# Two graph layers on Trainium2: layer 1's target factor moves from the values into ScalarE's exponential of the adjacency, head by head

## The chip, the cores and the metric

One core of one Trainium2 chip runs the whole program. The metric is the device time of one execution in microseconds. A profile is one further execution, recorded instruction by instruction; its span is the time from the first to the last recorded instruction. TensorE multiplies matrices, ScalarE applies functions and copies, VectorE and GpSimd work element by element, SyncE (SP) issues most of the transfers.

## The reference: what is computed

There are 64 graphs of 256 nodes with 512 features. Two layers of attention follow each other; "layer 0" is the first, and the second layer holds two attentions, here called "layer 1" (8 heads) and "layer 2" (1 head).

```python
# layer 0
scores = einsum('bihd,bjhd->bhij', Q, K) / 8 + a[i] + c[j] + log(adjacency + 1e-9)
x = softmax(scores) @ V + x
# layer 1 and layer 2, each on a normalised input
h = layer_norm(x) @ W
s, t = h . a_src, h . a_dst                  # one number per node and head
e = leaky_relu(s[i] + t[j], 0.2) + adjacency
x = softmax(e) @ h + x
```

With the leaky slope 0.2, exp(e) can be written as a product. Up to a factor that depends on the row i alone, and that the softmax divides out, it is `max(exp(-0.8 s_i), exp(0.8 t_j)) * exp(0.2 t_j) * exp(adjacency_ij)`. The first factor is called R (one row per head, the same on all partitions), `exp(0.8 t)` is called f, and `exp(0.2 t)` is the target factor.

## The kernel before, in words

**Tiles.** Targets j lie on the partitions, in two halves (NT = 2, 128 each), and sources i along the free axis (256). Weights of four heads make one tile `ET` of 128 x 2 x 4 x 256 (line 664); each graph makes two for layer 0 (`scores0`, lines 565 to 584) and two for layer 1 (lines 662 to 673). All share the tag `ET` with four buffers. A fresh pair for layer 1 therefore takes the buffers that "product 0" gives back, the product of layer 0's weights and values of the graph behind it.

**Order of the work.** `graph(b)` (line 456) is a generator; each `yield` closes a step. The lists `start`, `period` and `finish` (lines 752 to 825) put the steps of neighbouring graphs into one written order, in which up to six graphs are under way. TensorE follows this order to the letter (`manual_schedule` for PE, line 831). VectorE, ScalarE, GpSimd and SP get their order when the program is built, from a scheduler; once built it is fixed, and each engine takes its instructions strictly one after the other.

**Products with fixed weights** go through `winograd` (lines 293 to 343): seven products instead of eight, in three PSUM banks a, b and c. The order is product 1 into a, 5 into b, 2 into c, 6 added to a, 3 added to b, 7 added to a, then 4. Before product 6 adds to a, ScalarE must have copied m (`m1`) out of a; before product 3 it must have copied `m5` out of b; before product 7 it must have copied `u2` out of a. For the query these copies are `keep_q` (line 539), two instructions each.

**Layer 1**, the stage of the change:
- "V1", "V1 7", "V1 4" (lines 615 to 640) make the values V1 and, in eight more columns per half, the numbers s and t (`ends`). The copies of V1 are scaled with `rstd`, which comes from `var` on VectorE (line 273) and a power on GpSimd (line 275).
- "rows 1" (lines 642 to 660): `target_rows` writes `exp(-0.8 s)` to DRAM and loads it back on all partitions as two tiles R of four heads (512 KB each, line 452, two buffers). ScalarE makes f, and the target factors `exp(0.2 t)` in `factors` (line 650). VectorE multiplies V1 by them (line 657).
- eight steps "weights" (lines 669 to 673), one per head: VectorE computes `max(R, f) * EA` into ET, where `EA = exp(adjacency)` comes ready-made from line 497.
- "sums 1": `weight_sums` (line 359). The weights are summed over the targets by TensorE. Since they lack the target factor, the left operand holds the factors, and each half of the targets needs its own matmul: 4 rounds x 2 halves x 4 heads = 32 matmuls (line 370), each in a quarter of the array's columns. The reciprocal (line 377) goes to DRAM and back, spread over the partitions.
- "product 1", "gather 1": `weigh` (line 392) multiplies weights and scaled values (line 403), then VectorE applies the reciprocal and adds (lines 412, 417).

**Layer 0** in "sums 0" calls `weight_sums` too, with a sum of both halves made by VectorE first (line 599) and a left operand of ones: 16 matmuls.

**Layer 2** ("rows 2", line 715) scales EA with its factor on ScalarE, in place, and its weights (line 720) are the last reader of EA. EA has four buffers. AT, the transposed adjacency plus 1e-9, has one and is used by layer 0's mask alone (line 594). The transposes of the adjacency are at line 480.

Of the kernel before, what the change touches and what calls it, by code (L numbers as in the profile page):

```python
# [9 lines left out]
F32 = mybir.dt.float32  # L10
AF = mybir.ActivationFunctionType
ALU = mybir.AluOpType
AX = mybir.AxisListType

P = 128
H = 8
# [4 lines left out]
def kernel(  # L21
# [24 lines left out]
    nc = tc.nc  # L46
    B, N, D = x.shape
    KC = D // P
    NT = N // P
    DH = D // H  # L50
# [29 lines left out]
    def sum_columns(name, n):  # L80
        t = const.tile([P, 24 + 32 * n], F32, name=name)
        nc.gpsimd.memset(t, 0.0)
        return t, t[:, 24:].rearrange("p (n c) -> p n c", c=32)[:, :, :8]

    ones, eights = sum_columns("ones", 1)
    nc.gpsimd.memset(eights, 1.0)

    factor_columns = [sum_columns(f"factors{i}", NT * H) for i in range(2)]
    filled = [None, None]

    sources = {}
    for heads in (H, 1):
# [10 lines left out]
    HD = D // 2  # L103
# [44 lines left out]
    with ExitStack() as main:  # L148
        data = main.enter_context(tc.tile_pool(name="data", bufs=1))
        work = main.enter_context(tc.tile_pool(name="work", bufs=2))  # L150
        small = main.enter_context(tc.tile_pool(name="small", bufs=2))
# [204 lines left out]
                nc.vector.tensor_reduce(worst, bad, AX.X, ALU.max)  # L356
                nc.vector.tensor_tensor(odd, odd, worst, ALU.max)

        def weight_sums(terms):

            pt = ps("su")
            for i in range(4):
                for term in terms:
                    for g in range(4):
                        columns, at, weights = term(2 * g + i // 2)
                        nc.tensor.matmul(  # L370
                            pt[32 * g : 32 * g + 32, :P], columns[:, at - 8 * i : at - 8 * i + 32],
                            weights[:, i % 2 * P : i % 2 * P + P],
                            start=(i == 0 and term is terms[0]),
                            stop=(i == 3 and term is terms[-1]),
                        )
            inverse = small.tile([P, P], F32, name="inverse", tag="inverse", bufs=1)
            nc.vector.reciprocal(inverse, pt[:, :P])  # L377

            kept = dram.tile([2 * H, P], F32, name="kept", tag="keptsums")
            nc.sync.dma_start(out=kept, in_=inverse.rearrange("(i r) n -> i r n", r=8)[:, 0, :])  # L380

            R = data.tile([P, 2, N], F32, name="R", tag="Rs", bufs=2)
            heads_of = kept.rearrange("(a q s) n -> a q (s n)", a=4, q=2)
            for a in range(4):
                nc.sync.dma_start(
                    out=R[32 * a : 32 * a + 32], in_=heads_of[a].partition_broadcast(32)
                )
            nc.vector.tensor_tensor(top[:, :P], top[:, :P], pt[:, :P], ALU.max)
            nc.gpsimd.tensor_tensor(added, added, inverse, ALU.add)  # L389
            return R  # L390

# [30 lines left out]
        def target_rows(st, heads, b):  # L422

            if heads == 1 and b == B - 1:

                e = small.tile([P, NT], F32, name="last_rows", tag="last_rows")
                nc.scalar.activation(e, st[:, :, 0, 0], AF.Exp, scale=-0.8)
                wide = data.tile([P, NT, P], F32, name="wide", tag="R1")
                nc.vector.tensor_copy(wide, e.unsqueeze(2).to_broadcast([P, NT, P]))
                pt = ps("row")  # L430
                for t in range(NT):
                    nc.tensor.matmul(
                        pt[:, t * P : (t + 1) * P], wide[:, t, :], ident, start=True, stop=True
                    )
                return [pt[:, :N].rearrange("p (h n) -> p h n", h=1)]
            e = sources[heads][b % len(sources[heads])]
            nc.scalar.activation(e[:, :, :heads], st[:, :, 0, :], AF.Exp, scale=-0.8)
            rows = small.tile([P, NT, 32], F32, name="rows", tag="rows", bufs=1)
            nc.vector.transpose(rows, e)
            kept = dram.tile([H, N], F32, name="kept", tag="kept")  # L440
            for a in range(4):
                nc.sync.dma_start(
                    out=kept.rearrange("h (t a r) -> a h t r", t=NT, a=4)[a, :heads],
                    in_=rows[32 * a : 32 * a + heads],
                )
            got = []
            for q in range(0, heads, 4):
                n = min(4, heads - q)
                R = data.tile(
                    [P, n, N], F32, name="R", tag="R" if n == 4 else "R1", bufs=2 if n == 4 else 1  # L450
                )
                nc.sync.dma_start(out=R, in_=kept[q : q + n, :].partition_broadcast(P))
                got.append(R)
            return got

        def graph(b):
# [26 lines left out]
            for t in (1, 0):  # L483
# [1 line left out]
                    xT[:, :, t * P : (t + 1) * P].rearrange("p k (a r) -> p a k r", a=4),  # L485
                    X.rearrange("p (a t) (k r) -> p t a k r", t=NT, k=KC)[:, t],
                )
            AT = data.tile([P, NT, N], F32, name="AT", tag="AT")
            EA = data.tile([P, NT, N], F32, name="EA", tag="EA", bufs=4)

            def turn_adj():
                for j in range(NT):
                    turn(
                        AT[:, j, :].rearrange("p (t a r) -> p a t r", t=NT, a=4),
                        A.rearrange("p (a t) (j r) -> p j a t r", t=NT, j=NT)[:, j],
                    )
                nc.scalar.activation(EA, AT, AF.Exp)  # L497
                nc.scalar.activation(AT, AT, AF.Identity, bias=eps)

            if b > 0:  # L500
# [85 lines left out]
            pair = [scores0(0)]  # L586
# [4 lines left out]
            totals = []  # L591
            for ET, tag in zip(pair, ("QT", "KT")):
# [6 lines left out]
                nc.vector.tensor_tensor(total, ET[:, 0], ET[:, 1], ALU.add)  # L599
                totals.append(total)  # L600
                yield
            R = weight_sums([lambda h: (ones, 24, totals[h // 4][:, h % 4])])
            xT = fetch(stored, "yT")
            yield

# [9 lines left out]
            V1 = values("V1", 2)  # L615
# [21 lines left out]
            ends = small.tile([P, NT, 2, H], F32, name="ends", tag="ends")  # L637
# [4 lines left out]
            R = target_rows(ends, H, b)  # L642
            targets = ends[:, :, 1, :]
            f = small.tile([P, NT, H], F32, name="f", tag="f")
            nc.scalar.activation(f, targets, AF.Exp, scale=0.8)

            factors, factors8 = factor_columns[b % 2]
            filled[b % 2] = b
            for j in range(NT):
                nc.scalar.activation(  # L650
                    factors8[:, j * H : (j + 1) * H, :],
                    targets[:, j].unsqueeze(2).to_broadcast([P, H, 8]), AF.Exp, scale=0.2,
                )
                for n in range(2):
                    v = V1[:, j, n, :HD].rearrange("p (h d) -> p h d", d=DH)
                    at = j * H + n * H // 2
                    nc.vector.tensor_tensor(
                        v, v, factors8[:, at : at + H // 2, :1].to_broadcast([P, H // 2, DH]), ALU.mult
                    )
            note(ends.rearrange("p t i h -> p (t i h)"))  # L660
            yield
            pair = []
            for q in range(2):
                ET = work.tile([P, NT, 4, N], F32, name="ET1", tag="ET", bufs=4)
                pair.append(ET)
                for h in range(4):
                    at = 4 * q + h
                    for j in range(NT):
                        nc.vector.scalar_tensor_tensor(  # L669
                            ET[:, j, h, :], R[q][:, h, :], f[:, j, at : at + 1], EA[:, j, :],  # L670
                            ALU.max, ALU.mult,
                        )
                    yield
            assert filled[b % 2] == b
            R = weight_sums([
                lambda h, j=j: (factors, 24 + 32 * (j * H + h), pair[h // 4][:, j, h % 4])
                for j in range(NT)
            ])
            xT = fetch(stored, "xT" if last else "zT")
            yield  # L680
            for _ in weigh(pair, V1, R, xT, folded["1"].column):
# [21 lines left out]
            ends = small.tile([P, NT, 2, 1], F32, name="ends2", tag="ends2")  # L703
# [5 lines left out]
            R = target_rows(ends, 1, b)  # L709
            f = small.tile([P, NT], F32, name="f2", tag="f2")  # L710
            nc.scalar.activation(f, ends[:, :, 1, 0], AF.Exp, scale=0.8)
            factor = small.tile([P, NT], F32, name="factor", tag="factor")
            nc.scalar.activation(factor, ends[:, :, 1, 0], AF.Exp, scale=0.2)
            for j in range(NT):
                nc.scalar.mul(EA[:, j, :], EA[:, j, :], factor[:, j : j + 1])
            note(ends.rearrange("p t i h -> p (t i h)"))
            yield
            ET = work.tile([P, NT, N], F32, name="ET2", tag="ET2", bufs=1)
            for j in range(NT):
                nc.vector.scalar_tensor_tensor(  # L720
                    ET[:, j, :], R[0][:, 0, :], f[:, j : j + 1], EA[:, j, :], ALU.max, ALU.mult
                )
            yield
            rinv = small.tile([P, NT], F32, name="rinv2", tag="rinv2")
# [372 lines left out]
```

## Time and profile before

| | |
|---|---|
| median of 3 runs | 3311.77 us (3309.73 to 3312.42) |
| span of the profiled execution | 3309.9 us |
| TensorE busy (matmul) | 3241.0 us, 98% |
| VectorE busy | 2434.1 us, 74% |
| ScalarE busy | 1453.7 us, 44% |
| GpSimd busy | 924.0 us, 28% |
| layer 1's weights (L669, VectorE) | 463.6 us, 1024 instructions |
| layer 1's sum matmuls (L370, factors) | 4096 |
| scaling of V1 (L657, VectorE) | 141.2 us, 256 instructions |

A line such as `L669 DVE ... ET<-R,f,EA ... x1024` names the source line, the engine (PE TensorE, PEld its weight load, DVE VectorE, ACT ScalarE, POOL GpSimd, SPq SyncE's queue), the tile written and those read, and how many instructions there were. In a timeline a row is one instruction or several like ones in sequence: start, length from the first start to the last end, engine, line, count; a bracket at the end gives the idle time before it and what ended it. Neighbours on one engine overlap a little, so the spacing of starts is shorter than the duration. Ends of matmuls are modelled; their starts are the better measure.

### The profile page before, as it was taken

To read this page: it belongs to the slowest core of one execution; us is meant where nothing else is said; L and a number is where in the kernel's file an instruction comes from. 1 tells how busy PE (TensorE), PEld (TensorE's weight loads), DVE (VectorE), ACT (ScalarE), POOL (GpSimd) and SP (SyncE) were. 2 spreads that over 40 slices of the span, in tenths; PEclk is the share of its full clock that TensorE was granted. 3 is DMA by queue.
4 is the path that set the end of the run, shared out by engine and by line. 5 is a ranking of instruction groups with operands and counts; after the bars stand their busy time and mean duration, and the time that the engine had idled before them with its cause. 6 is when DMAs were issued, how large, how long until landed. Compare 5 with 4: busy or idle time off the path is not lost.

```text
span 3309.9 us, 80363 instructions
## 1 busy us (share of the span) xinstructions
PE 3241.0 (98%) x31048; PEld 2745.3 (83%) x31048; DVE 2434.1 (74%) x5267; ACT 1453.7 (44%) x4039; POOL 924.0 (28%) x1246
## 2 busy tenths in 40 slices
PE   6899999999999999999999999999999999999997
PEld 4688888888888888888888888888888888888875
DVE  5677777777777777777777777777777777777776
ACT  2344444444444444444444444444444444444442
POOL 2232232232222322322322322322222223223222
PEclk9999999999999999999999999999999999999998
DMA  4323334334334333333333343343343333343322
GB/s 122 109 84 115 102 97 113 105 89 120 105 91 118 105 93 113 95 108 111 92 113 105 94 114 103 93 116 106 89 119 101 95 113 102 101 113 94 108 90 70
DMA packets 271667, 341.14 MB, mean 103 GB/s; under 512 B 108576, under 2 KB 187568, under 8 KB 271280
## 3 DMA queue, kind: packets, MB, share of 16 engines
q1 hardware_dynamic: 270512, 335.40, 35.4%
q8 instruction: 248, 4.06, 0.5%
q14 instruction: 139, 1.14, 0.1%
q10 hardware_dynamic: 768, 0.54, 0.1%
HBM read 233.48 MB, written 102.31 MB: 101 GB/s over the span
## 4 chain that ended last, share of the span: by engine, by line
PE 95%; DVE 2%; DMA 1%; SPq 1%; issue 1%; ACT 0%; POOL 0%; ACTq 0%; DVEq 0%; POOLq 0%
PE ps_a L309 21%; PE ps_a L316 13%; PE ps_num L403 13%; PE ps_b L309 10%; PE ps_b L316 7%; PE ps_sc L573 7%; PE ps_av L732 7%; PE ps_su L370 6%; PE ps_c L309 5%; PE ps_tr L252 4%; PE ps_c L316 3%; SPq L120 1%; DVE ET L669 0%; POOL product L180 0%; DMA kept<-inverse 0%
## 5 line engine op out<-in xcount | busy, mean ns | idle before, releaser
L669 DVE SCALAR_TENSOR_TENSOR ET<-R,f,EA 128x256 f32<-128x256 f32 x1024 | 463.6, 518 | 135.8 <-PE ps_num L403 134.5
L403 PE MATMUL ps_num<-ET,V 128*32 128x256 f32 x8192 | 465.9, 379 | 0.0
L403 PEld LDWEIGHTS ps_num<-ET,V 128*32 128x32 f32 x8192 | 263.5, 110 | 154.9 <-issue 0.8
L594 DVE TENSOR_TENSOR ET<-ET,AT 128x1024 f32<-128x1024 f32 x256 | 304.2, 1222 | 108.3 <-ACT ET L580 108.3
L580 ACT ACTIVATE ET<-ps_sc,V 128x512 f32<-128x512 f32 x512 | 303.3, 703 | 102.1 <-PE ps_sc L573 88.9
L389 POOL TENSOR_TENSOR added<-added,inverse 128x128 f32<-128x128 f32 x128 | 69.9, 546 | 921.7 <-DVE inverse L377 764.3
L309 PE MATMUL ps_a<-w,S 128*128 128x264 f32 (+1 forms) x1024 | 273.3, 389 | 0.9 <-ACT m L618 0.9
L309 PE MATMUL ps_b<-w,S 128*128 128x264 f32 (+1 forms) x1024 | 266.6, 383 | 0.0
L285 POOL TENSOR_TENSOR S<-yT 128x256 f32<-128x256 f32 x64 | 66.1, 1033 | 670.2 <-PE ps_su L370 595.6
L732 PE MATMUL ps_av<-V,ET 128*128 128x258 f32 (+1 forms) x1024 | 245.5, 383 | 7.2 <-DVE ET L720 7.2
L573 PE MATMUL ps_sc<-QT,KT 64*128 64x256 f32 x2048 | 238.6, 383 | 0.0
L309 PEld LDWEIGHTS ps_a<-w,S 128*128 128x128 f32 x1024 | 187.0, 189 | 51.0 <-issue 19.9
L573 PEld LDWEIGHTS ps_sc<-QT,KT 64*128 64x128 f32 x2048 | 192.7, 187 | 40.7 <-issue 20.3
L309 PEld LDWEIGHTS ps_b<-w,S 128*128 128x128 f32 x1024 | 193.8, 189 | 31.4 <-issue 0.4
L732 PEld LDWEIGHTS ps_av<-V,ET 128*128 128x128 f32 x1024 | 186.5, 192 | 30.3 <-issue 6.2
L412 DVE TENSOR_TENSOR ps_num<-ps_num,R 128x512 f32<-128x512 f32 x256 | 165.8, 692 | 59.0 <-DMA R<-kept 57.3
L690 POOL TENSOR_TENSOR X<-X,bw 128x512 f32<-128x512 f32 x128 | 159.9, 1271 | 162.3 <-ACT X L267 162.3
L269 ACT ACTIVATE ps_tr<-ps_tr,less 128x512 f32<-128x512 f32 x256 | 165.9, 648 | 0.0
L309 PE MATMUL ps_a<-wv,xT 128*128 128x257 f32 x512 | 142.1, 400 | 21.9 <-ACT ET L580 11.2
L497 ACT ACTIVATE EA<-AT 128x512 f32<-128x512 f32 x64 | 40.4, 632 | 280.1 <-DVE ET L720 263.6
L599 DVE TENSOR_TENSOR total<-ET 128x1024 f32<-128x1024 f32 x128 | 153.7, 1201 | 0.0
L309 PE MATMUL ps_a<-wv,S 128*128 128x257 f32 x512 | 135.2, 387 | 8.9 <-ACT m L506 5.0
(168 smaller groups left out, 6933.7 us busy)
## 6 DMA issues: line engine op xcount, KB each, us to landing
R<-kept SPq DMA_DIRECT2D x128, 512.0 KB
X<-in_x_dram SPq DMA_DIRECT2D x256, 128.0 KB
kept<-xT SPq DMA_DIRECT2D x64, 512.0 KB
yT<-kept SPq DMA_DIRECT2D x64, 512.0 KB
R<-kept SPq DMA_DIRECT2D x512, 64.0 KB
kept<-yT SPq DMA_DIRECT2D x64, 512.0 KB
out_dram<-X SPq DMA_DIRECT2D x512, 64.0 KB
zT<-kept SPq DMA_DIRECT2D x63, 512.0 KB
```

Of the source, the lines that this page charges most:

```text
L269: nc.scalar.activation(pt, pt, AF.Square, bias=less[:, of], accum_out=squares[:, of])
L309: nc.tensor.matmul(to, A[:, kk, :], B[:, kk, :], start=(first and kk == 0), stop=(kk == 1), skip_group_check=not first,)
L316: nc.tensor.matmul(to[:, m * P : (m + 1) * P], B[:, kk, m * P : (m + 1) * P], A[:, kk, :], start=(first and m == kk == 0), stop=(kk == 1), ...
L370: nc.tensor.matmul(pt[32 * g : 32 * g + 32, :P], columns[:, at - 8 * i : at - 8 * i + 32], weights[:, i % 2 * P : i % 2 * P + P], start=(i ...
L403: nc.tensor.matmul(num[32 * a : 32 * a + 32, m * N : (m + 1) * N], V[:, j, a // 2, a % 2 * P + q * DH + 32 * m :][:, :32], pair[a // 2][:, ...
L412: nc.vector.tensor_tensor(both, both, R[:, q, :].unsqueeze(1).to_broadcast([P, 2, N]), ALU.mult)
L573: nc.tensor.matmul(banks[h % 2][:, o : o + N], KT[lo : lo + DH, (q + h) // 2, j * P : (j + 1) * P], QT[lo : lo + DH, (q + h) // 2, :], sta ...
L580: nc.scalar.activation(ET[:, j, i::2, :], banks[i].rearrange("p (h n) -> p h n", n=N), AF.Exp, bias=c[:, j, :],)
L594: nc.vector.tensor_tensor(ET[:, j, :, :], ET[:, j, :, :], AT[:, j, :].unsqueeze(1).to_broadcast([P, 4, N]), ALU.mult,)
L669: nc.vector.scalar_tensor_tensor(ET[:, j, h, :], R[q][:, h, :], f[:, j, at : at + 1], EA[:, j, :], ALU.max, ALU.mult,)
L690: nc.gpsimd.tensor_tensor(X2[t], X2[t], folded["2"].row, ALU.add)
L732: nc.tensor.matmul(av[:, :width], ET[:, j, t * P : (t + 1) * P], V2[:, j, n, :width], start=(j == 0), stop=(j == NT - 1),)
```

## The change

The target factor `exp(0.2 t)` leaves the values and the left operand of the sums. `0.2 t` becomes a small tile `lift`, and ScalarE computes `exp(adjacency + lift)` for each head and each half of the targets, 16 instructions per graph, straight into ET; VectorE's weights then read and write ET in place. With the factor in the weights, both halves can be added first: VectorE does that after the fourth and the eighth head, into the tile R that has just been used up, and `weight_sums` takes these totals with the left operand of ones. R gets a third buffer, and now is held until the sums have read it. EA goes; AT gets four buffers, since it is now kept until layer 2, where ScalarE puts the exponential in AT's place.

```diff
-    factor_columns = [sum_columns(f"factors{i}", NT * H) for i in range(2)]
-    filled = [None, None]
...
-        def weight_sums(terms):
+        def weight_sums(totals):
             pt = ps("su")
             for i in range(4):
-                for term in terms:
-                    for g in range(4):
-                        columns, at, weights = term(2 * g + i // 2)
-                        nc.tensor.matmul(
-                            pt[32 * g : 32 * g + 32, :P], columns[:, at - 8 * i : at - 8 * i + 32],
-                            weights[:, i % 2 * P : i % 2 * P + P],
-                            start=(i == 0 and term is terms[0]),
-                            stop=(i == 3 and term is terms[-1]),
-                        )
+                for g in range(4):
+                    h = 2 * g + i // 2
+                    nc.tensor.matmul(
+                        pt[32 * g : 32 * g + 32, :P], ones[:, 24 - 8 * i : 24 - 8 * i + 32],
+                        totals[h // 4][:, h % 4, i % 2 * P : i % 2 * P + P],
+                        start=(i == 0), stop=(i == 3),
+                    )
...
                 R = data.tile(
-                    [P, n, N], F32, name="R", tag="R" if n == 4 else "R1", bufs=2 if n == 4 else 1
+                    [P, n, N], F32, name="R", tag="R" if n == 4 else "R1", bufs=3 if n == 4 else 1
                 )
...
-            AT = data.tile([P, NT, N], F32, name="AT", tag="AT")
-            EA = data.tile([P, NT, N], F32, name="EA", tag="EA", bufs=4)
+            AT = data.tile([P, NT, N], F32, name="AT", tag="AT", bufs=4)
...
-                nc.scalar.activation(EA, AT, AF.Exp)
                 nc.scalar.activation(AT, AT, AF.Identity, bias=eps)
...
-            R = weight_sums([lambda h: (ones, 24, totals[h // 4][:, h % 4])])
+            R = weight_sums(totals)
...
-            factors, factors8 = factor_columns[b % 2]
-            filled[b % 2] = b
-            for j in range(NT):
-                nc.scalar.activation(
-                    factors8[:, j * H : (j + 1) * H, :],
-                    targets[:, j].unsqueeze(2).to_broadcast([P, H, 8]), AF.Exp, scale=0.2,
-                )
-                for n in range(2):
-                    v = V1[:, j, n, :HD].rearrange("p (h d) -> p h d", d=DH)
-                    at = j * H + n * H // 2
-                    nc.vector.tensor_tensor(
-                        v, v, factors8[:, at : at + H // 2, :1].to_broadcast([P, H // 2, DH]), ALU.mult
-                    )
+            lift = small.tile([P, NT, H], F32, name="lift", tag="lift")
+            nc.vector.tensor_scalar(lift, targets, 0.2, None, ALU.mult)
...
                     for j in range(NT):
+                        nc.scalar.activation(
+                            ET[:, j, h, :], AT[:, j, :], AF.Exp, bias=lift[:, j, at : at + 1]
+                        )
                         nc.vector.scalar_tensor_tensor(
-                            ET[:, j, h, :], R[q][:, h, :], f[:, j, at : at + 1], EA[:, j, :],
+                            ET[:, j, h, :], R[q][:, h, :], f[:, j, at : at + 1], ET[:, j, h, :],
                             ALU.max, ALU.mult,
                         )
+                    if h == 3:
+                        nc.vector.tensor_tensor(R[q], ET[:, 0], ET[:, 1], ALU.add)
                     yield
-            assert filled[b % 2] == b
-            R = weight_sums([
-                lambda h, j=j: (factors, 24 + 32 * (j * H + h), pair[h // 4][:, j, h % 4])
-                for j in range(NT)
-            ])
+            R = weight_sums(R)
...
-            factor = small.tile([P, NT], F32, name="factor", tag="factor")
-            nc.scalar.activation(factor, ends[:, :, 1, 0], AF.Exp, scale=0.2)
+            lift = small.tile([P, NT], F32, name="lift2", tag="lift2")
+            nc.vector.tensor_scalar(lift, ends[:, :, 1, 0], 0.2, None, ALU.mult)
             for j in range(NT):
-                nc.scalar.mul(EA[:, j, :], EA[:, j, :], factor[:, j : j + 1])
+                nc.scalar.activation(AT[:, j, :], AT[:, j, :], AF.Exp, bias=lift[:, j : j + 1])
...
-                    ET[:, j, :], R[0][:, 0, :], f[:, j : j + 1], EA[:, j, :], ALU.max, ALU.mult
+                    ET[:, j, :], R[0][:, 0, :], f[:, j : j + 1], AT[:, j, :], ALU.max, ALU.mult
```

## The prediction

> **What bounds the kernel now.** First I read the busy times and the chain that ended last.
>
> ```profile
> PE 3241.0 (98%) x31048; PEld 2745.3 (83%) x31048; DVE 2434.1 (74%) x5267; ACT 1453.7 (44%) x4039; POOL 924.0 (28%) x1246
> ...
> PE 95%; DVE 2%; DMA 1%; SPq 1%; issue 1%; ACT 0%; POOL 0%; ACTq 0%; DVEq 0%; POOLq 0%
> ```
>
> TensorE ends nearly every step; other engines matter only where they keep it waiting. In the list of the chain's pieces the same `ps_sc` piece returns every 50.18 us (1501.90, 1552.08): one graph. So I read the timeline of one graph, from 1501 us, on TensorE, ScalarE and VectorE (start, length, engine, line).
>
> ```profile
> 1512.62 1.08 PE L370 MATMUL ps_su<-total,ones 128*32 128x128 f32 x32
> 1513.52 3.64 PE L403 MATMUL ps_num<-ET,V 128*32 128x256 f32 x64
> 1517.08 1.14 PE L309 MATMUL ps_a<-wv,xT 128*128 128x257 f32 x4
> ...
> 1520.73 1.06 PE L316 MATMUL ps_a<-S,wq 128*128 128x128 f32 x8
> 1521.62 1.06 PE L316 MATMUL ps_b<-S,wq 128*128 128x128 f32 x8
> 1522.52 1.15 PE L316 MATMUL ps_a<-S,wq 128*128 128x128 f32 x8
> 1523.60 1.95 PE L370 MATMUL ps_su<-ET,factors 128*32 128x128 f32 x64
> 1525.37 3.64 PE L403 MATMUL ps_num<-ET,V 128*32 128x256 f32 x64
> ```
>
> Starts follow each other without a gap. The sums of layer 1 (x64) hold TensorE 1525.37 - 1523.60 = 1.77 us; those of layer 0 (x32) 1513.52 - 1512.62 = 0.90.
>
> ```profile
> 1513.94 0.91 ACT L715 ACTIVATE EA<-EA,factor 128x256 f32<-128x256 f32 x2
> ...
> 1518.25 0.38 ACT L516 COPY V<-ps_a 128x257 f32<-128x257 f32 x1 [3.41 <-PE ps_a L309]
> 1519.15 0.63 ACT L539 ACTIVATE m<-ps_a,columns 128x128 f32<-128x128 f32 x2 [0.52 <-PE ps_a L316]
> 1520.04 0.63 ACT L539 ACTIVATE m<-ps_b,columns 128x128 f32<-128x128 f32 x2 [0.27 <-PE ps_b L316]
> 1521.83 0.63 ACT L539 ACTIVATE u<-ps_a,columns 128x128 f32<-128x128 f32 x2 [1.16 <-PE ps_a L316]
> ```
>
> Here is the tight place. The query's seventh Winograd product adds to bank `ps_a` at 1522.52, so ScalarE must have copied `u` out of it: that ends at 1521.83 + 0.63 = 1522.46. The spare is 0.06 us. For `m` it is almost 1 us each.
>
> ```profile
> 1517.19 4.05 DVE L669 SCALAR_TENSOR_TENSOR ET<-R,f,EA 128x256 f32<-128x256 f32 x10 [2.20 <-PE ps_num L403]
> ...
> 1532.52 0.17 DVE L273 TENSOR_SCALAR var<-squares 128x2 f32<-128x2 f32 x1
> ```
>
> The weights start at 1517.19, when product 0 (`ps_num`, from 1513.52) releases its two ET buffers. `var` matters below. Two rows by form give durations:
>
> ```profile
> L715 ACT ACTIVATE EA<-EA,factor 128x256 f32<-128x256 f32 x128 | 58.1, 501 | 2.0
> ...
> L657 DVE TENSOR_TENSOR V<-V,factors 128x256 f32<-128x256 f32 x256 | 141.2, 609 | 0.0
> ```
>
> **What the Trainium skill says.** "ScalarE: Activation LUTs", What ACT_TABLE_LOAD costs: with a bias pointer an activation takes about 280 ns + 0.833 ns per element, back to back 93 ns overlap, the same for every function. For 256 elements: 493 ns, then one per 0.40 us. The trace agrees for a pointer operand (501 ns; the pair takes 0.91, so the second adds 0.41); it shows no exponential of this shape. "TensorEngine Tiling (Array Packing)", Key Properties: changing the tiling mode drains TensorE. The seventh product's slot, 1.08 us against 0.89 for its neighbours, fits this; the change keeps the number of switches. "DMA: Bandwidth & Descriptors", Queues, rings and completion order: descriptors of one queue are consumed in order but aren't held back for one another; so a load issued before a store should mostly go first. This trace doesn't show such a pair.
>
> **TensorE.** Sixteen sum matmuls fewer per graph: 1.77 - 0.90 = 0.87 us off, since the remaining 16 have layer 0's form. All else keeps its order.
>
> **ScalarE.** It loses one exponential of 128x512 (632 ns) and two factor exponentials (241 ns); layer 2's two scalings become two exponentials of the same shape, costed at nothing. It gains 16 exponentials of 128x256: 16 x 0.40 = 6.4 us. ScalarE is busy 22.7 us of 50.2, so there is room; place decides. The changed program, as built, puts all 16 behind the pair of layer 2, and the first waits for the same ET release, 1517.2. Its order from there: three exponentials, the V copy, one, the pair m, one, the second m, four, the pair u, seven. Behind each exponential thus stand copies for TensorE. Up to the end of u: 9 x 0.405 + 0.29 + 3 x 0.54 + 0.09 = 5.65 us (0.29 and 0.54 are 0.38 and 0.63 less the overlap). So u ends at 1522.85, not 1522.46, and the seventh product waits **0.39 us**. The m's end at 1519.8 and 1520.7, before products six and three (1520.73, 1521.62) want them. Bounds: at 0.37 us each (the slope of L539, 128 elements, to L580, 512, both read from PSUM) the wait is about 0.1; with no overlap, 0.50 each, 1.25. I take 0.405, between page and pair.
>
> **VectorE.** It loses four scalings of V, 141.2 / 64 = 2.2 us, and gains two target sums (L599's form, 1.20 each, 1.13 back to back) and two tiny `lift`s (below 0.3 each, by L273's mean of 294 ns): about +0.7 us on an engine with 12 us free. The place again: nine weights and both sums now stand after layer 1's reciprocal, ahead of or around `var`. Each of the first seven weights follows its exponential; the seventh ends issuing at 1522.0. Then, by the spacings of before: `ps_num` 1.20, yT 1.56, layer 2's weights 0.79, QT 0.34, turn of A 0.69, QT 0.34, reciprocal 0.86, maximum 0.15: 1527.9; eighth weight 1528.3.
>
> The ninth needs the second half of R. Its load (512 KB) moves: with three buffers it now waits for the sums of the graph before, end 1523.60 + 0.39 + 0.90 = 1524.9, where SP issued it at 1503.8. On SP the yT store, A's loads, the inverse's store and R's four loads queue behind this wait; the yT store could go only at 1524.7, so at most 0.2 us is lost. The last chain in the tail has a 512 KB load at 3.75 us (zT), the start one at 4.20 (R). With 3.75 it lands at 1528.65. Then ninth weight 0.41, sum 1.13, three weights 1.22, rinv 0.15, a weight 0.41, L739 0.48, var 0.17: 1532.6, before 1532.69. From var's end GpSimd's rstd and ScalarE's m took until 1534.12, 1.43 us: now 1534.05. TensorE's sixth product of V1 stood at 1535.16 and is now at 1535.16 - 0.87 + 0.39 = 1534.68. Spare: 0.6 us, which also covers VectorE's weights beside GpSimd (three took 2.14 us at 1527.91, 1.26 at 1521.49). Cost: nothing, while the load lands within 4.3 us.
>
> The later zT update, about 1540.6, stays ahead of TensorE's transposes (1542.30 - 0.48). AT's four buffers only put the turn behind layer 2's weights on the same engine.
>
> **Sum.** Per regular graph -0.87 + 0.39 = -0.48 us. The built order shows 58 like periods: -27.8 us. The remaining starting and ending graphs I count as no gain, and +2 us at the end, where a first exponential (0.5) and a sum or two (1.2 each) enter a chain of VectorE. 3309.9 - 27.8 + 2 = 3284; the median of runs lies 1.9 above the profiled span: **3286 us**.
>
> **Rivals.**
> **A, the late load (slower).** Load and yT store share the engines and both finish late. The store moved data from 1526.25 to 1527.8; shared fully, the load takes 3.75 + 1.55 = 5.3 us, 1.0 past the spare. Then -0.48 + 1.0 = +0.5 x 58 + 2: 3343. It ends slower beyond 4.8 us. For: the start's 4.20 is already near. Against: the load is first on its queue.
> **B, slower exponentials.** At 0.455 each the wait is 0.84, and the gain is gone: 3312. Fully without overlap: 3336. Against: the 0.41 pair.
> **C, no wait.** The exponentials fit, all 0.87 stays: -50 + 0: 3261. For: it needs only 0.04 us less per exponential. Against: the spare is just 0.06.
> The edit does what it says; the built order leaves no doubt there.
>
> **How the numbers follow.** Forecast 0.45, A 0.28, B 0.15, C 0.12. The forecast's own range is 3275 to 3298; with A and C down to 1 in 10 each side, 3258 to 3345. About 0.2% (6.6 us) is what can be told apart. Faster: 0.43 + 0.12 = 0.55. Same: most of B and the forecast's edge, 0.14. Slower: A and the worst of B, 0.31.
>
> **What would show it.** The profile after: 0.90 us from the sums of layer 1 to product 1; a wait of TensorE's L316 `ps_a` on ScalarE's u near 0.4 us per graph; exponentials 0.40 apart; a period near 49.7 us. A wait of TensorE on V1's m, or of VectorE's ninth weight on R for over a microsecond, is rival A. No wait at u is C. I am wrong if a queue I held covered, SP's R loads or the tail, ends a wait.

## The result, and the profile after

The changed kernel takes a median of 3303.43 us (3300.73 to 3306.52, 10 runs) against 3312.39 us (3309.42 to 3313.54, 10 runs) for the kernel before: ratio 0.9975, 95% interval [0.9966, 0.9984]. It is faster by 9 us, where 26 were forecast. Its profiled span is 3303.0 us, before 3309.9, so the two traces differ by 6.9 us, and that is the sum to be explained.

The busy times and the chain that ended last, of the changed kernel:

```profile
PE 3208.0 (97%) x29000; PEld 2686.9 (81%) x29000; DVE 2488.2 (75%) x5267; ACT 1761.0 (53%) x4807; POOL 899.5 (27%) x1244
...
PE 80%; ACT 10%; DVE 3%; DMA 3%; issue 2%; SPq 1%; POOL 1%; ACTq 0%; DVEq 0%; POOLq 0%
```

TensorE has 2048 matmul records fewer (32 a graph: the profile records each of the 16 matmuls as two), but its share of the chain fell from 95 to 80%. ScalarE holds 10% of the path now, DMA 3%. Before, it was 0% and 1%.

The list of the chain's pieces (start, length, what) of the changed kernel gives the length of each graph's period, from one `ps_sc` to the next:

```profile
353.02 3.65 PE ps_sc L562 x32
...
402.69 3.65 PE ps_sc L562 x32
...
425.86 4.85 DMA R<-kept
452.85 3.65 PE ps_sc L562 x32
...
502.68 3.65 PE ps_sc L562 x32
...
526.13 5.54 DMA R<-kept
553.80 3.65 PE ps_sc L562 x32
```

Before, every regular period was 50.18 us. Now they are 49.67 (402.69 - 353.02), 50.16, 49.83, 51.12. Over the 56 periods from the scores of graph 4 to those of graph 60 the shortest is 49.67, the mean 49.89, the longest 51.20. In the eleven of them over 50 us, and in no other, a piece `DMA R<-kept` stands in the chain. No regular period of before has one.

A period without a late load, on TensorE (the same stretch as was shown of before, now at 1461 us):

```profile
1461.18 1.08 PE L362 MATMUL ps_su<-total,ones 128*32 128x128 f32 x32
1462.08 3.64 PE L394 MATMUL ps_num<-ET,V 128*32 128x256 f32 x64
...
1470.19 1.06 PE L313 MATMUL ps_b<-S,wq 128*128 128x128 f32 x8
1471.44 1.16 PE L313 MATMUL ps_a<-S,wq 128*128 128x128 f32 x8 [0.20 <-ACT u L528]
1472.53 1.08 PE L362 MATMUL ps_su<-R,ones 128*32 128x128 f32 x32
1473.43 3.64 PE L394 MATMUL ps_num<-ET,V 128*32 128x256 f32 x64
```

Layer 1's sums hold TensorE 1473.43 - 1472.53 = 0.90 us, before 1.77. The seventh product starts 1.25 us after its neighbour (1471.44 - 1470.19) where before it was 0.90; from product 0 to layer 1's sums it is 10.45 us, before 10.08: 0.37 us lost. Here is what stands before the copy of u on ScalarE:

```profile
1465.81 1.31 ACT L647 ACTIVATE ET<-AT,lift 128x256 f32<-128x256 f32 x3 [2.70 <-PE ps_num L394]
1467.03 0.35 ACT L505 COPY V<-ps_a 128x257 f32<-128x257 f32 x1
1467.28 0.51 ACT L647 ACTIVATE ET<-AT,lift 128x256 f32<-128x256 f32 x1
1467.71 0.62 ACT L528 ACTIVATE m<-ps_a,columns 128x128 f32<-128x128 f32 x2
1468.22 0.51 ACT L647 ACTIVATE ET<-AT,lift 128x256 f32<-128x256 f32 x1
1468.66 0.63 ACT L528 ACTIVATE m<-ps_b,columns 128x128 f32<-128x128 f32 x2
1469.18 1.70 ACT L647 ACTIVATE ET<-AT,lift 128x256 f32<-128x256 f32 x4
1470.77 0.61 ACT L528 ACTIVATE u<-ps_a,columns 128x128 f32<-128x128 f32 x2
```

Nine exponentials, 0.40 us apart, and the copy of u ends at 1471.38. It had ended 0.06 us before the product wanted it; now the product, due at 1471.08 (0.89 behind its neighbour), waits for it.

And the longest period, whose scores begin at 1798.87 us. First SP's queue, then VectorE, then TensorE:

```profile
1822.12 0.34 SPq L443 DMA_DIRECT2D R<-kept  x1
1822.50 0.43 SPq L236 DMA_DIRECT2D kept<-yT  x1
```

```profile
1825.48 0.74 DVE L650 SCALAR_TENSOR_TENSOR ET<-R,f,ET 128x256 f32<-128x256 f32 x1
1828.03 0.49 DVE L650 SCALAR_TENSOR_TENSOR ET<-R,f,ET 128x256 f32<-128x256 f32 x1 [1.81 <-DMA R<-kept]
1828.44 1.22 DVE L655 TENSOR_TENSOR R<-ET 128x1024 f32<-128x1024 f32 x1
...
1831.62 0.16 DVE L270 TENSOR_SCALAR var<-squares 128x2 f32<-128x2 f32 x1
```

```profile
1830.81 1.05 PE L306 MATMUL ps_c<-w,yT 128*128 128x264 f32 x4
1833.12 1.16 PE L306 MATMUL ps_a<-w,S 128*128 128x264 f32 x4 [1.25 <-ACT m L607]
```

The load goes out at 1822.12 and the yT store 0.38 us behind it. The ninth weight starts at 1828.03, so the load took 5.91 us. `var`, queued behind it on VectorE, comes late, then rstd, then the copy m, and TensorE's sixth product of V1 waits. From issue to ninth weight, called the landing from here on, I read all 56 periods: at most 4.04 us in the best nine, where the weight hardly waited or not at all, a median of 4.55, at most 5.91. The period follows as 49.67 + (landing - 4.41), where that is above zero, within 0.02 us in 54 of the 56: here 49.67 + 1.50 = 51.17, measured 51.20.

Where the 6.9 us come from, by the starts of the scores in both traces:

| stretch | before | after | difference |
|---|---|---|---|
| span's start to scores of graph 4 | 247.4 | 253.4 | +6.0 |
| 56 periods at the shortest length | 2809.9 | 2781.5 | -28.4 |
| their excess over it (late loads) | 0 | 12.2 | +12.2 |
| scores of graph 60 to the end | 252.6 | 255.8 | +3.2 |

Together -7.0, measured -6.9. My theory: the regular graph was forecast rightly, and the gain was given back at three places: the late R, the start and the end. The rivals: the late load stands only beside a VectorE that is overloaded anyway, and the 0.37 us at the seventh product stems from something else than the exponentials.

### The profile page after: what moved, and what is told of

Its sections match the earlier page's. It is cut to its first block, busy times and chain, and to the rows that moved or that the text cites. A ratio compares the mean times of both kernels' runs of the same rounds, so it can differ in the third digit from the quotient of the medians.

```text
span 3303.0 us, 76975 instructions
## 1 busy us (share of the span) xinstructions
PE 3208.0 (97%) x29000; PEld 2686.9 (81%) x29000; DVE 2488.2 (75%) x5267; ACT 1761.0 (53%) x4807; POOL 899.5 (27%) x1244
## 4 chain that ended last, share of the span: by engine, by line
PE 80%; ACT 10%; DVE 3%; DMA 3%; issue 2%; SPq 1%; POOL 1%; ACTq 0%; DVEq 0%; POOLq 0%
PE ps_a L306 18%; PE ps_num L394 12%; PE ps_a L313 10%; PE ps_b L306 9%; PE ps_sc L562 7%; PE ps_av L711 6%; ACT ET L647 6%; PE ps_c L306 4%; PE ps_su L362 4%; PE ps_b L313 3%; PE ps_tr L249 3%; ACT m L528 2%; DMA R<-kept 2%; PE ps_c L313 2%; ACT u L528 1%
## 5 line engine op out<-in xcount | busy, mean ns | idle before, releaser
L650 DVE SCALAR_TENSOR_TENSOR ET<-R,f,ET 128x256 f32<-128x256 f32 x1024 | 468.3, 496 | 243.4 <-ACT ET L647 214.7
L647 ACT ACTIVATE ET<-AT,lift 128x256 f32<-128x256 f32 x1024 | 442.6, 505 | 172.0 <-PE ps_num L394 172.0
L380 POOL TENSOR_TENSOR added<-added,inverse 128x128 f32<-128x128 f32 x128 | 60.1, 470 | 891.7 <-DVE inverse L368 891.7
L282 POOL TENSOR_TENSOR S<-yT 128x256 f32<-128x256 f32 x64 | 54.5, 851 | 626.2 <-PE ps_su L362 556.9
L272 POOL TENSOR_TENSOR rstd<-var,mhalf 128x2 f32<-128x2 f32 x128 | 90.6, 708 | 284.7 <-DVE var L270 278.2
L282 POOL TENSOR_TENSOR S<-zT 128x256 f32<-128x256 f32 x63 | 45.8, 727 | 445.5 <-DVE zT L408 419.2
```

Of the source, the lines that this page charges most:

```text
L647: nc.scalar.activation(ET[:, j, h, :], AT[:, j, :], AF.Exp, bias=lift[:, j, at : at + 1])
L650: nc.vector.scalar_tensor_tensor(ET[:, j, h, :], R[q][:, h, :], f[:, j, at : at + 1], ET[:, j, h, :], ALU.max, ALU.mult,)
```

## Experiments

Each kernel is timed against the kernel before on the same chip, whose medians there were 3311.5 to 3311.8 us.

**R with four buffers.** Both loads go out early again. A tile of the set-up moves to another place to make the room.

```diff
-  ... tag="R" if n == 4 else "R1", bufs=3 if n == 4 else 1
+  ... tag="R" if n == 4 else "R1", bufs=4 if n == 4 else 1
-  sums = data.tile([P, HD + H], F32, name="sums", tag="sums")
+  sums = data.tile([P, HD + H], F32, name="sums", tag="R1")
```

> R has four buffers instead of three, so that both of its loads go out early again, as in the kernel before, and not behind the sums of the graph before. Theory late load (the second half of R lands a median 4.55 us after its issue where 4.41 are free, and TensorE pays the excess in most periods): every regular period falls to the shortest seen, 49.67 us, instead of a mean of 49.89, so 56 x 0.215 = 12 us go and the time is about 3291 us (3287 to 3295). Rival theory, that the excess comes from elsewhere (VectorE simply has too much to do ahead of var) and the load is only late beside it: periods keep a mean near 49.9 and the time stays within 3300 to 3306 us.

Measured: 3293.22 us, ratio 0.9945 [0.9931, 0.9958]. The periods have a mean of 49.69 and a median of 49.68 us: all but 1 of the 12 us of excess is gone, as the late-load theory says, and VectorE's order of work up to `var` is unchanged. The waits view of VectorE for R (us in total, times, longest), first the changed kernel, then this one:

```profile
DVE ET L650 <- DMA R<-kept: 28.4, 51, 2.8
```

```profile
DVE ET L650 <- DMA R<-kept: 3.6, 2, 3.0
```

From 51 waits (28.4 us) to 2. The overloaded VectorE falls as a rival.

**The store moved behind.** The late load stays; the yT store that followed it at once goes out some microseconds later, behind the last load of the spread reciprocal.

```diff
             left = left_factors(xT, "yS")
-            stored = store(xT)
             yield
             rstd = rstd_of(xT)
+            with tc.issue_after(last_load[0].ins):
+                stored = store(xT)
```

> The changed kernel's late load of R stays where it is, but the yT store of 512 KB, which was issued 0.4 us behind it, moves a few microseconds later on the same queue, so that the load has the DMA engines to itself. Theory shared engines: the load lands within 4.1 us in all periods, the waits of VectorE's ninth weight fall inside the 4.41 us that are free, periods are 49.67 us and the time about 3291 us (3287 to 3295). Rival, that such a load takes 4.0 to 5.9 us by itself: landings keep a median near 4.55 us, and the time stays near 3303 us (3299 to 3307).

Measured: 3295.51 us, ratio 0.9952 [0.9938, 0.9966]; periods of mean 49.72, median 49.68. The same period as above, whose scores begin at 1792.21 here:

```profile
1815.46 0.34 SPq L445 DMA_DIRECT2D R<-kept  x1
1817.13 0.34 SPq L465 DMA_DIRECT2D A<-in_adj_dram  x1
...
1822.36 0.45 SPq L236 DMA_DIRECT2D kept<-yT  x1
```

```profile
1819.68 0.48 DVE L653 SCALAR_TENSOR_TENSOR ET<-R,f,ET 128x256 f32<-128x256 f32 x1 [0.52 <-DMA R<-kept]
```

4.22 us instead of 5.91, in one of the eight periods where VectorE still waited; inside the 4.41 that are free. The trace's packet records say the same: with nothing behind it, R's 128 packets of 4 KB had ended a median of 3.40 us after the issue (3.11 to 4.48). With the store behind it, the 256 packets of both ended at a median of 5.42, and the first half of these bytes, R's or the store's, at 3.54. So the first half of the bytes arrives about as fast as R does alone; since the weight waits longer, it can't be all R's (the records don't name the transfer). Sharing is the cause, and R is not slow by itself. The forecast that all landings would be early failed: five of the 56 are over 4.41, the latest at 5.12, and 2 us of excess remain.

**The exponentials behind u.** From the fourth head on they stand behind the second copy of the query's u; this sets the order on ScalarE, and is no wait on a semaphore.

```diff
+                        if at == 3 and j == 0:
+                            behind = copied[-1].ins.name
+                        if at >= 3:
+                            tc.add_manual_dep(made.ins, behind, ...)
```

> The fourth and later pairs of ScalarE's exponentials are held behind the copy of the query's u, so that six stand before it instead of nine. Theory: the 0.38 us wait of the query's seventh product in each graph is those exponentials, and nothing else is late there: the wait is gone, the shortest period is 49.29 us, and 58 x 0.38 = 22 us go: about 3281 us (3277 to 3287), with the late load of R still costing what it did. Rival: another latecomer takes the wait's place (a copy of m, or VectorE's weights, which now start later for the second half and push var back): 3292 to 3305 us.

Measured: 3278.70 us, ratio 0.9903 [0.9888, 0.9918]. TensorE and ScalarE in a period whose scores begin at 1438.79:

```profile
1458.59 1.06 PE L313 MATMUL ps_b<-S,wq 128*128 128x128 f32 x8
1459.53 1.16 PE L313 MATMUL ps_a<-S,wq 128*128 128x128 f32 x8
1460.62 1.08 PE L364 MATMUL ps_su<-R,ones 128*32 128x128 f32 x32
```

```profile
1457.58 0.51 ACT L651 ACTIVATE ET<-AT,lift 128x256 f32<-128x256 f32 x1
1458.85 0.63 ACT L530 ACTIVATE u<-ps_a,columns 128x128 f32<-128x128 f32 x2 [0.76 <-PE ps_a L313]
```

ScalarE is idle for 0.76 us before u, and the product comes 0.94 us after its neighbour. The shortest period is 49.36, so 0.31 of the 0.37 us came back; 0.06 stay, and why stays open. The time fell by more than the 56 x 0.31 = 17 us of this: the excess from the late R fell too, from 12 to 4 us (mean 49.44). That I had not expected. In the new order VectorE makes an update of X (L718 in the changed kernel) behind `var` and no longer ahead of it. From the ninth weight to `var` it takes a median of 3.19 us, in the changed kernel 3.58, so the load has 0.4 us more. This fits; it was not tested by itself.

**Both mends.**

> Four buffers for R and the exponentials held behind the copy of u, together. If the two causes (late load, 0.215 us a period; exponentials ahead of u, 0.38 us) are separate and complete, the regular period is 49.29 us throughout and the time 3303.4 - 12 - 22 = about 3269 us (3264 to 3275). If one hides behind the other, or a third latecomer stands close behind them, 3275 to 3292 us.

Measured: 3277.57 us, ratio 0.9898 [0.9883, 0.9913]. Periods of mean 49.40, shortest 49.36. This is not to be told from the last kernel by its time. The reason is that most of the late R had gone there already. The forecast of 3269 failed by 8.6 us: the shortest period is 0.07 us longer than I reckoned (4 us over 56 periods), and 2 us of excess over it remain; the rest is not explained. The two ends are as slow as in the changed kernel: 253.0 us to the scores of graph 4, 256.7 from those of graph 60, against 247.4 and 252.6 before the change.

**ScalarE's part alone.**

```diff
-  R = weight_sums(R)
+  R = weight_sums([[pair[0][:, j], pair[1][:, j]] for j in range(NT)])
...
-  if h == 3:
-      nc.vector.tensor_tensor(R[q], ET[:, 0], ET[:, 1], ALU.add)
...
-  ... bufs=3 if n == 4 else 1
+  ... bufs=2 if n == 4 else 1
```

> ScalarE's part of the change alone: the target factor goes into the exponentials, the values stay unscaled, but VectorE adds no target tiles; layer 1's sums take both halves on TensorE with the column of ones, 32 matmuls as before the change, and R keeps its two buffers and early loads. Theory: the exponentials ahead of the copy of u cost 0.37 us in each of 58 regular graphs and nothing takes it back: the regular period is 50.18 + 0.37 = 50.55 us, the time 3312 + 21 = about 3333 us (3329 to 3338). Rival, that the wait at the query's seventh product stems from the other parts of the change (shorter sums, later R): about 3312 us.

Measured: 3335.03 us, ratio 1.0069 [1.0055, 1.0083]. Every period is 50.55 us:

```profile
1484.75 1.16 PE L313 MATMUL ps_a<-S,wq 128*128 128x128 f32 x8 [0.20 <-ACT u L530]
1485.84 1.95 PE L363 MATMUL ps_su<-ET,ones 128*32 128x128 f32 x64
```

The same wait at u, with the long sums and early loads: 0.37 us a graph belong to the exponentials alone.

**TensorE's part alone.** The kernel before, with layer 1's sums over the first half of the targets alone; the second half is left out, so these are not the sums of the reference.

```diff
             R = weight_sums([
                 lambda h, j=j: (factors, 24 + 32 * (j * H + h), pair[h // 4][:, j, h % 4])
-                for j in range(NT)
+                for j in range(1)
```

> TensorE's part of the change alone, in the kernel before: layer 1's sums leave out the terms of the second target tile (so they are not the sums of the reference), 16 matmuls in place of 32; scaling, exponentials and loads are as before the change. Theory: TensorE's 0.87 us a graph is all on the path, and no other engine is close behind: the regular period is 50.18 - 0.87 = 49.31 us, the time 3312 - 64 x 0.87 = about 3256 us (3253 to 3262). Rival, that shorter sums meet a latecomer of their own (R for VectorE, the rstd of V1, a start that is bound by something else): 3262 to 3285 us.

Measured: 3259.70 us, ratio 0.9841 [0.9828, 0.9855]. The period is 49.30, that is 0.87 less, as reckoned. But the median fell by 52 us and not 56, the profiled span by 49: 48 of it in the regular stretch; up to the scores of graph 4 it is 1.0 us, from those of graph 60 on 0.1. At the ends shorter sums bring next to nothing.

**The start.** On the kernel with both mends: GpSimd's four products of the second weight's fold stand ahead of graph 2's sums, as before the change (`behind` is the fold's last product and given for graph 2 alone; `first` and `third` are two of the four sums S).

```diff
+  if behind is not None:
+      for op in (first, third):
+          tc.add_manual_dep(op.ins, behind.ins.name, ...)
```

> The kernel with four R buffers and the exponentials behind u, and in the start GpSimd's four products for folding the second weight are put ahead of the sums of graph 2's x, as they stood in the kernel before. Theory: the start's loss of some 6 us against the kernel before begins there (VectorE's adds of V1 of graph 0 stood behind the fold's reductions, which waited for GpSimd: TensorE's wait for them rose from 1.9 to 4.1 us); the scores of graph 4 begin at about 250 us instead of 253.0, the time is about 3274 us (3272 to 3276). Rival, that the start is bound by loads (SP's queue, on which the weights of W2 stand later than before) and the wait only moves: scores of graph 4 at 252 to 254 us, the time 3276 to 3280 us.

Measured: 3274.29 us, ratio 0.9885 [0.9870, 0.9900]. The scores of graph 1 begin at 99.6 us, as before the change (99.7), where the kernel with both mends has 102.5. But of these 2.9 us only 1.5 reach the scores of graph 4 (251.5): TensorE's next wait, for ScalarE's copy of u of graph 2's values, grew from 4.8 to 6.7 us. The theory named the first loss; the wait moved on, as the rival had it, though to ScalarE's copy and not to loads. ScalarE's part alone already has the slow start: there the scores of graph 1 begin at 102.2 us, those of graph 4 at 250.5.

**The end.** On the kernel with both mends: the last two graphs sum both halves on TensorE.

```diff
-                    if h == 3:
+                    if h == 3 and b < B - 2:
...
-            R = weight_sums(R)
+            if b < B - 2:
+                R = weight_sums(R)
+            else:
+                R = weight_sums(*([ET[:, j] for ET in pair] for j in range(NT)))
```

> The kernel with four R buffers and the exponentials behind u; for the last two graphs VectorE adds no target tiles, and TensorE sums both halves (32 matmuls) instead. Theory: in the tail TensorE has nothing else to do while the totals are added, and its 7.1 us of waits for them (3.4 and 3.7 us) shrink by the 1.2 us of a total or two each, less 2 x 0.87 us of longer sums: the end comes 1 to 3 us sooner, 3275 to 3277 us. Rival, that the weights themselves (the exponential's chain) are what is late: no change or 1 us slower, 3277 to 3280 us.

Measured: 3272.68 us, ratio 0.9880 [0.9865, 0.9895]; from the scores of graph 60 to the end 250.3 us instead of 256.7. TensorE's waits for layer 1's sums in this stretch, with the totals and without:

```profile
PE ps_su L364 <- DVE R L669: 7.1, 2, 3.7
```

```profile
PE ps_su L365 <- DVE ET L666: 2.6, 2, 1.4
```

More than I forecast (1 to 3 us): by the medians the totals cost 4.9 us. In the traces it is 6.4 us, of which 4.5 lie between the products before these sums and those behind (from 3215.77 to 3235.24 with the totals, from 3214.61 to 3229.59 without). The exponentials are not what is slow there: ScalarE's part alone, which makes no totals, takes 252.5 us from the scores of graph 60, as before the change (252.6).

**Both ends mended, and one step more in the start.**

> The two mends at the ends together: GpSimd's fold products ahead of graph 2's sums in the start, and no target tiles added by VectorE for the last two graphs; four R buffers and the exponentials behind u as well. If the two are apart in time they add up: 3277.6 - 3.3 - 4.9 = about 3269 us (3267 to 3272). If the gain of one was in truth the run's scatter: 3272 to 3276 us.

Measured: 3266.67 us, ratio 0.9868 [0.9850, 0.9886]; the two add up (3269 was forecast). The next kernel puts graph 0's exponentials (`made`) and the eps shift of graph 3's adjacency behind the copy of u of graph 2's values as well:

```diff
+  if b == 0 and at > 0:
+      behind_v(made)
...
+  if b == 3:
+      behind_v(shift)
```

> As the last one, and in the start graph 0's exponentials after the first pair, and the eps shift of graph 3's adjacency, stand behind ScalarE's copy of u for graph 2's values. Theory: what the start still loses between the scores of graphs 1 and 2 (52.4 us, before the change 45.3) is TensorE's wait of 6.7 us for that copy, which stands behind work that waits for R; with it in front, the scores of graph 2 begin at 146 to 149 us instead of 152.0 and the time is 3263 to 3267 us. Rival: the wait moves on to VectorE's adds of those values, which stand behind weights that wait for the same R: 3267 to 3271 us.

Measured: 3266.78 us, ratio 0.9864 [0.9847, 0.9882]: no gain. The copy is early, but the wait moved, not to VectorE's adds as the rival had it, but to a chain of loads of the fold:

```profile
117.78 0.24 PE L229 MATMUL ps_fold<-ident,chunks 4*128 4x4 f32 x1 [8.98 <-DMA chunks<-bw]
```

At this place TensorE now waits for a transfer. The start also varies: kernels with the same order of the start, one with both mends and one with the end mended besides, had the scores of graph 4 at 253.0 and 251.8 us, the two with the fold's products moved at 251.5 and 248.4, and the one with four R buffers alone at 250.4. Most of this is TensorE's granted clock: in the two with the products moved, the same matmuls, from 37 us to the scores of graph 4, took 181.6 us at a mean clock of 0.91, and 179.0 at 0.94. The end varies too, by 2 us between the last two kernels (250.5 and 252.5), whose edits there are the same. So the start's +6.0 us is known to about 3 us, and its split among its waits stays open. Both last kernels are some 37 us faster than the changed kernel, and 45 faster than the kernel before.

## Why the prediction was wrong

**The sums (0.87 us off): right.** 1.77 to 0.90, and alone it shortens the period by 0.87.

**ScalarE (0.39 us of wait at u): right.** Nine exponentials 0.40 us apart, 0.37 us measured, and the exponentials alone give the same. Rivals B and C fall with it. The forecast of -0.48 a graph is nearly the shortest period's -0.505; 58 such graphs were reckoned, and 56 counted here, so the sum comes out close.

**The late load: the step that failed.** "With 3.75 it lands at 1528.65 ... Cost: nothing, while the load lands within 4.3 us." The limit was right (4.41). The landing was mis-sized, and its cost with it, which was put at nothing: a median of 4.55 instead of 3.75, and spread from below 4.03 to 5.91. I had taken one transfer of the tail as the duration, and held the store behind it harmless because the load is first on its queue. That is what rival A said would go wrong, and the moved store shows its mechanism. But A's price of 1.0 us a graph was for full sharing each time; it cost 0.215 on average, 12 us in all. So the truth lay between the forecast and A: a landing that spreads around its limit costs the mean of its excess, not all or nothing. The Trainium skill's "DMA: Bandwidth & Descriptors" says, under "Two DMAs through the same engine are not ordered", that descriptors of one queue start in order but are pipelined. The traces fit this and don't show it packet by packet: issued 0.38 us apart, load and store together ended at a median of 5.42 us, and the load, which alone had ended at 3.40, was waited for until 4.55 (medians). "Mostly go first", as I read it, was not enough with 0.6 us to spare.

**The ends: the second miss.** "The remaining starting and ending graphs I count as no gain, and +2 us at the end." No gain was right (1.1 us with the short sums alone). The end cost 3.2: two totals of 1.2 us stand before TensorE's sums with nothing to hide them. The start was counted at nothing and cost about 6. There the scheduler's new order put GpSimd's fold products behind graph 2's sums: in the kernel before they started at 90.06 us, in the changed one at 95.07. VectorE, in its fixed order, had the fold's reductions ahead of the adds of V1, which TensorE needs. Moving the products back brought 1.5 us at the scores of graph 4 (3.3 us by the medians); the rest of the start's loss stays open, though part of it is the granted clock of the last section.

Forecast and measurement by terms: regular periods -27.8 (measured -28.4), late loads 0 (+12.2), start 0 (+6.0), end +2 (+3.2).

## What to carry to other kernels

A duration read from one transfer is no bound where the spare is of its own size: take what else the same step releases on that queue, and cost the spread around the limit. An instruction moved to an idle engine is paid by what stands behind it in that engine's order; here the order alone was worth 0.31 us a graph. And work that hides in the regular stretch may not hide where the pipeline fills and drains: the totals cost about 5 us at the end, which wants a form of its own.

## What the runs showed that I had not expected

A wait of TensorE in the start cost more than its length. In the changed kernel, and in the kernel before, the product after the wait and the 32 score matmuls behind it:

```profile
101.49 2.13 PE L306 MATMUL ps_a<-w,yT 128*128 128x264 f32 x4 [4.06 <-DVE V L616]
103.55 5.09 PE L562 MATMUL ps_sc<-QT,KT 64*128 64x256 f32 x32
```

```profile
98.64 1.16 PE L309 MATMUL ps_a<-w,yT 128*128 128x264 f32 x4 [1.88 <-DVE V L627]
99.73 3.73 PE L573 MATMUL ps_sc<-QT,KT 64*128 64x256 f32 x32
```

After 4.06 us of waiting both took longer, by 0.97 and 1.36 us; after 1.88 us they didn't. The table by stretches (window, length, busy times of PE, PEld, DVE, ACT, POOL, then granted clock) gives the reason, first two rows of the changed kernel, then one of before:

```profile
102.00:105.00 3.00, 3.00 (x12) 1.87 (x12) 2.08 (x3) 0.48 (x1) 2.33 (x2) 0.50 0.16 23
105.00:108.00 3.00, 3.00 (x24) 2.56 (x22) 1.42 (x4) 2.34 (x6) 0.00 (x0) 0.78 0.55 195
```

```profile
102.00:105.00 3.00, 3.00 (x46) 1.89 (x42) 3.00 (x6) 3.00 (x6) 0.00 (x0) 1.00 0.20 79
```

The granted clock was 0.50 and 0.78; before, in the same windows, 1.00, as in all of 95 to 108 us. So the 2.2 us by which the wait grew became about 4.5.

The Trainium skill's "TensorE: Matmul & The Clock Gate", Part 1: The HAM clock gate (What's actually happening), gives half rate after an idle window of about 3.4 us. These two waits fit that, but the traces show no sharp limit in the length of a wait. The same product, the sixth of graph 2's V1, waited 2.60 us in the kernel of "The start" and 2.67 us in the one with the store moved behind:

```profile
185.35 2.13 PE L317 MATMUL ps_a<-w,S 128*128 128x264 f32 x4 [2.60 <-ACT m L622]
```

```profile
185.69 1.16 PE L306 MATMUL ps_a<-w,S 128*128 128x264 f32 x4 [2.67 <-ACT m L610]
```

Behind the shorter wait the granted clock was 0.53 from 185 to 188 us, behind the longer one 1.00. What decides it for waits of this length stays open.
